# Order of the convolution units and of ScalarE's waits in a convolution-attention-Mamba kernel

## Chip, cores, metric

The kernel runs on one core of a Trainium2 chip. The metric is the device time of one execution in microseconds (us). Engines are named as in the profile: PE (TensorE), DVE (VectorE), ACT (ScalarE), POOL (GpSimd) and SP (SyncE, which here only issues DMAs).

## What is computed

The input is one image of 64 x 64 points with 256 channels. Layer 0 normalises it by groups and computes three convolutions, q, k and v, each followed by a depthwise 3 x 3 convolution; attention over the 4096 points in 8 heads follows. Layer 1 treats the points as tokens: a Mamba block in both directions with a small two-layer network behind it, and then two of eight experts, chosen from the mean of all tokens.

```python
qkv = concat([conv(xc, W1, 0), conv(xc, W3, 1), conv(xc, W5, 2)], axis=1)   # 1x1, 3x3, 5x5
qkv = conv(qkv, Wdw, 1, groups=3 * c)                                       # depthwise 3x3
q, k, v = split(qkv, 3)
q, k = l2n(q), l2n(k)                     # each row of 4096 points is divided by its norm
attn = softmax(q @ k.T * temperature)
...
h = dA_t * h + dBx_t                      # Mamba: for each token, 512 x 16 states, both directions
y = sum_s(h * C_t)
y = (y + xc * Dp) * silu(z)
```

The norm `l2n` runs over the 32 channels of a head at each point. In Mamba dA = exp(dt * A), dBx = dt * B * xc, and z is the second half of the input projection.

## The kernel before

**Three stages matter here**: `conv_phase` (0 to about 682 us), `attention_phase` (to about 1990) and `mamba_phase` (to about 3890); the experts come last. In the first and the third the order of the instructions on each engine is the order in which the program text issues them: nothing reorders them later, and each engine takes its own in order. What runs beside what is therefore decided by where generators are stepped.

**Convolutions.** k and v are Winograd-like convolutions along x: `inputs` (DVE) combines shifted columns of the padded input into transformed planes v0 to v8 ("places", nine of them, taken and freed), `weights` (DVE) combines the raw weights of one row dy into transformed weights in three pieces (two for k), stores them by DMA from POOL into `uv` or `uk`, and PE multiplies. q is 1 x 1 and needs no transform. The work goes by units (kind, half of the image, tile of 128 channels), in the order of the list `units`. Four PSUM buffers (`cv`) hold products; `feed` issues products on PE, up to three ahead of `product`, which hands them out.

For a k or v unit `transform_out` takes the products in pairs: ACT copies the second to `c`, DVE adds and subtracts into `out_t` and combines the rest into `pad`, one of two padded images (a unit uses `pads[n % 2]`). For q `evacuate` copies four products into `pad` on ACT. `sides` then copies the outer columns. `depthwise` of a unit runs while the next unit is made: ACT does tap 0 (L541), DVE the other eight taps of two pieces (L548, 16 instructions). v's result is transposed by PE (`turn`, L612) and copied out by ACT (L614). q's and k's go in sets of three chunks through `norm_sums` (ACT squares, PE sums), `norm_inverse` (DVE reciprocal, 3.35 us, and PE spreading it) and `norm_apply` (DVE), one step for each `tick`. The first half of the image leaves nine rows for the second in `edges`.

In the unit loop each group does, in this order: a step of the unit's own work, `feed`, `tick`, some steps of the depthwise before it, and `share[kind]` steps of `step_fill`, which advances the list `fills`: inputs and weights of k and v that are still to be made. `fills[5]` is `all_weights("v", 1)`: five rows dy in three pieces, 15 pieces.

**Mamba.** There are 16 steps (8 chunks of 512 tokens, two directions), each with 32 slots. A slot n handles two groups of 32 channels times 4 states: POOL makes `dbx` (`inflow`, L1713), ACT makes `da` (`decay`, L1703), DVE scans (`recur`, L1724) and multiplies by C (L1729; in five of 32 slots POOL does it, L1734), PE sums (`sum_states`, L1761), and ACT keeps the last column (`keep`, L1752). In each slot the loop issues `inflow(n + 2)`, `keep(n - 1)`, `decay(n + 1)`, `bring(n + 1)`, `recur(n)`.

A scan covers two channel groups in one instruction, so the state that enters the second is added by `bring` (L1744), a one-column ACT instruction on `dbx`, from `brought`. `carry` makes `brought` in three parts: POOL (L1437), ACT's exp (L1439), POOL (L1442); for the first half of a step in slots 30 and 31 of the step before, for the second in slots 9 to 11. L1437 reads `first_r`, which `load_first` (L1427) loads by DMA through SP from a row (`first_row`, L1414) that `dt_piece` stored. In slot 8 there is one `bring` more, for slot 10:

```python
bring(n + 1)
if at == 8:
    bring(n + 2)
```

`prepare(q)` makes all inputs of step q while step q - 1 runs, one generator step a slot; its last six steps fall into slots 24 to 29. There `zs` (two PSUM tiles of the input projection) is copied to `z` on ACT (L1398), both tiles in slot 24 and both in slot 26, and `load_first(q, 0)` is issued in slot 28, after the second `first_row` store.

Of the kernel before, what the change touches and what calls it, by code (L numbers as in the profile page):

```python
# [14 lines left out]
FP = mybir.dt.float32  # L15
# [9 lines left out]
P = 128  # L25
# [4 lines left out]
N = 512  # L30
# [143 lines left out]
def conv_phase(cx, xT, w1, w3, w5, temp, qd, kd, vd, uk, uv):  # L174
# [13 lines left out]
    nc, tc = cx.nc, cx.tc  # L188
    HR = 32
    LAG = 24  # L190
    TX = W // 4
    with ExitStack() as ctx:
        one = ctx.enter_context(tc.tile_pool(name="a_one", bufs=1))
# [24 lines left out]
        for pad in pads:  # L218
            nc.gpsimd.memset(pad[:, :, 0, 0], 0.0)
            nc.gpsimd.memset(pad[:, :, 5, TX - 1], 0.0)  # L220
        edges = {k: one.tile([P, 9, 6, TX], FP, name=f"edge{i}") for i, k in enumerate((0, 1, "q"))}
        out_t = one.tile([P, 4 * N], FP, name="out_t")
        wq = one.tile([P, CT, C], FP, name="wq")
        for t in range(CT):
# [185 lines left out]


        units = [("k", h, t) for h in range(2) for t in range(CT)]
        units += [("q", 0, 0), ("v", 0, 0), ("v", 0, 1), ("q", 1, 0), ("q", 0, 1), ("q", 1, 1), ("v", 1, 0), ("v", 1, 1)]
        jobs = [
            (u, i) for u in units for i in (range(4) if u[0] == "q" else PTS[u[0]])
        ]
# [1 line left out]
        at = {"load": 0, "job": 0, "used": 0}  # L418
# [81 lines left out]
            yield  # L500

        def sides(pad, r0):
            nc.scalar.copy(pad[:, r0 : r0 + HR, 0, 1:TX], pad[:, r0 : r0 + HR, 4, 0 : TX - 1])
            nc.scalar.copy(pad[:, r0 : r0 + HR, 5, 0 : TX - 1], pad[:, r0 : r0 + HR, 1, 1:TX])

        diag = one.tile([P, 9, P], FP, name="diag")

# [14 lines left out]
        def depthwise(kind, half, t, pad):  # L522

            row0, n = (LAG, H - LAG) if half else (0, LAG)
            ch = {"q": 0, "k": CT, "v": 2 * CT}[kind] + t
            dst = accp.tile([P, (H - LAG) * W], FP, name="acc", tag="acc")
            shared = 16 if (kind, half, t) == units[-1] else 0
            mine = n - shared

            def piece(b, tap):  # L530
                dy, dx = divmod(tap, 3)
                m = mine // 2
                return (
                    dst[:, m * W * b : m * W * (b + 1)].rearrange("p (h w) -> p h w", w=W),
                    pad[:, m * b + dy : m * b + dy + m, dx : dx + 4, :].rearrange("p h s j -> p h (s j)"),
                    wdw[:, 9 * ch + tap : 9 * ch + tap + 1],
                )

            for b in range(2):
                o, src, w_ap = piece(b, 0)  # L540
                nc.scalar.activation(o, src, AF.Copy, scale=w_ap)  # L541
            parts = [pcv.tile([P, N], FP, name="cv", tag="cv") for _ in range(shared // 8)]
            for i, ps in enumerate(parts):
                products(pad, mine + 8 * i, ps)
            for b in range(2):
                for tap in range(1, 9):
                    o, src, w_ap = piece(b, tap)
                    nc.vector.scalar_tensor_tensor(o, src, w_ap, o, ALU.mult, ALU.add)  # L548
                    yield
                if kind == "v":  # L550
                    m = mine * W // P // 2
                    turn(dst, t, row0 * W // P, m * b, m)
                if b == 0 and shared:
                    for i, ps in enumerate(parts):
                        nc.scalar.copy(dst[:, W * (mine + 8 * i) : W * (mine + 8 * i + 8)], ps)
                    turn(dst, t, row0 * W // P, 2 * m, shared * W // P)
            if kind != "v":
                c0 = row0 // ROWS
                rows_left.extend((dst[:, N * j : N * j + N], kind, t, c0 + j) for j in range(n // ROWS))
                if not busy:  # L560
                    norm_sums()

        def norm_sums():

            chunks = rows_left[:3]
            del rows_left[:3]
            busy[:] = chunks
            if not chunks:  # L570
                return
            ps = pms.tile([P, N], FP, name="ps", tag="ps0")
            for j, (a, _, _, _) in enumerate(chunks):
                sq = tp.tile([P, N], FP, name="sq", tag="t")
                nc.scalar.activation(sq, a, AF.Square)
                nc.tensor.matmul(ps[32 * j : 32 * j + 32, :], heads, sq, start=True, stop=True)
            later(lambda: norm_inverse(chunks, ps))
# [44 lines left out]
        def tick():  # L622

            clock[0] += 1
            due = [f for n, f in events if n <= clock[0]]
            events[:] = [(n, f) for n, f in events if n > clock[0]]
            for f in due:
                f()

        with tc.manual_schedule(engines=ORDERED):  # L630
# [68 lines left out]

            pure = fills[1::2]  # L700

            def step_fill():


                held = False
                for f in list(fills):
                    if held and f not in pure:
                        continue
                    r = next(f, None)
                    if r:  # L710
                        return True
                    if r is None:
                        fills.remove(f)
                    else:
                        held = True
                return False


            share = {"k": 5, "q": 4, "v": 3}
            before = None  # L720
            for n, (kind, half, t) in enumerate(units):
                pad, r0 = pads[n % 2], 9 if half else 1
                edge = edges["q" if kind == "q" else t]
                if half:
                    nc.scalar.copy(pad[:, 0:9], edge)
                    nc.gpsimd.memset(pad[:, HR + 9, :, :], 0.0)
                else:
                    nc.gpsimd.memset(pad[:, 0, :, :], 0.0)
                if kind == "q":
                    def evacuate():  # L730
                        for i in range(4):
                            r = r0 + 16 * (i // 2)
                            nc.scalar.copy(
                                pad[:, r : r + 16, 1 + 2 * (i % 2) : 3 + 2 * (i % 2), :],
                                product().rearrange("p (h s j) -> p h s j", s=2, j=TX),
                            )
                        sides(pad, r0)
                        yield

                    main, groups = evacuate(), 1  # L740
                else:
                    main, groups = transform_out(kind, pad, r0), len(PTS[kind]) // 2
                if n == 0:
                    feed()
                    for _ in range(6):
                        step_fill()
                for g in range(groups):
                    step(main)
                    feed()
                    tick()  # L750
                    for _ in range(-(-18 // groups)):
                        step(before)
                    for _ in range(share[kind]):
                        step_fill()
                    feed()
                drain(main)
                drain(before)
                if not half:
                    nc.scalar.copy(edge, pad[:, LAG : LAG + 9])
                before = depthwise(kind, half, t, pad)  # L760
                if n == len(units) - 2:
                    diagonal(2 * CT + units[-1][2])
# [441 lines left out]
def mamba_phase(cx, early, w_in, w_x, w_out, w1, w2, x1d, ud, bcd, dtd, x2d, u2d, usum):  # L1204
# [11 lines left out]
    nc, tc = cx.nc, cx.tc  # L1216
    with ExitStack() as ctx:
# [87 lines left out]
        def prepare(q):  # L1305
# [78 lines left out]
            yield  # L1384
            got["dt"] = dt
            for at, (v, e) in enumerate(((0, 0), (1, 0), (0, 1), (0, 2), (0, 3), (1, 1))):
                dt_piece(q, v, e, ex)
                if at == 4 and q > 1:
                    load_first(q, 0)
                if at == 1:  # L1390
                    zs = in_pair(q, ET + 2)
                    if q + 1 < 2 * NCH:
                        load_u(q + 1)
                if at in (0, 2):
                    z = sp.tile([P, 2, N], FP, name="z", tag="z", bufs=3)
                    got.setdefault("z", []).append(z)
                    for f in range(2):
                        nc.scalar.copy(z[:, f, :], zs[f])  # L1398
                yield

        def dt_piece(q, v, e, ex=None, eng=nc.gpsimd):
# [21 lines left out]
        def load_first(q, h):  # L1423

            t_ = got_first[q, h] = ip.tile([P, 4, 2], FP, name="first_r", tag="first_r", bufs=1)
            rows = first_rows.pop((q, h)).rearrange("(c j) e -> c (j e)", j=4)
            nc.sync.dma_start(out=t_.rearrange("p j e -> p (j e)"), in_=rows[:, None].to_broadcast([32, 4, 8]))  # L1427
# [361 lines left out]
        with tc.manual_schedule(engines=ORDERED):  # L1789
# [5 lines left out]
            for n, (i, e, k, j) in enumerate(slots):  # L1795
# [8 lines left out]
                if n > 0:  # L1804
                    decay(n + 1)
                bring(n + 1)
                if at == 8:
                    bring(n + 2)
                recur(n)
                nxt = (i, e + 1) if e < ET - 1 else (i + 1, 0)  # L1810
                if nxt[0] < 2 * NCH:
# [377 lines left out]
```

## Time and profile before

| | |
|---|---|
| median of 3 runs (lowest, highest) | 4211.03 us (4209.73, 4214.56) |
| profiled execution | 4214.29 us, span 4212.5 us |
| mean granted PE clock | 0.925 |
| PE busy | 3616.6 us (86%) |
| DVE busy | 3493.8 us (83%) |
| ACT busy | 2678.3 us (64%) |
| POOL busy | 1739.0 us (41%) |

The span is from the first to the last instruction of the profiled execution; its own time is 1.8 us longer. Busy shares are means over stages with different limits, so they say little alone: a wait counts only where the waiting engine is the one that sets the pace of its stage. In the profile a group is named by its line and by the tiles written and read ("acc<-pad"); idle time is put down to the instruction that ended it ("<-PE ps L576").

### The profile page before, as it was taken

How to read it: one execution, taken by the hardware profiler on the slowest of the kernel's cores; microseconds unless marked ns; L12 is line 12 of the kernel's file. 1: busy time of each engine (PE TensorE's matmuls, PEld its weight loads, DVE VectorE, ACT ScalarE, POOL GpSimd, SP SyncE). 2: the span in 40 equal slices, each digit the busy share in tenths (PEclk: the TensorE clock that was granted, in tenths of full speed). 3: DMA queues.
4: the chain of work that ended last, by engine and by line, in shares of the span. 5: the costliest groups of instructions: out<-in, count | busy, mean ns of one | idle time of the engine just before them, and what ended most of it. 6: DMA issues, size and time to landing. Idle time of an engine off the chain costs nothing. (4 is left out here: it accounts for less than half of the span.)

```text
span 4212.5 us, 43554 instructions
## 1 busy us (share of the span) xinstructions
PE 3616.6 (86%) x15116; PEld 1182.8 (28%) x15116; DVE 3493.8 (83%) x2898; ACT 2678.3 (64%) x4187; POOL 1739.0 (41%) x1132
## 2 busy tenths in 40 slices
PE   6679698999999999998788788878888888875798
PEld 2223242222222222222222222322222222221343
DVE  8996767879879878778899999999999999999211
ACT  1111315878878878776777777777777777774122
POOL 3200000000000000001888888888888888886000
PEclk9889798999999999999888899989899999977899
DMA  6412124000000000002334343443334443442121
GB/s 208 133 62 89 42 80 140 9 29 19 16 24 19 17 24 19 11 21 85 111 117 122 117 128 114 132 121 117 118 106 128 121 128 117 134 114 72 65 65 39
DMA packets 150532, 351.19 MB, mean 83 GB/s; under 512 B 35493, under 2 KB 44453, under 8 KB 150046
## 3 DMA queue, kind: packets, MB, share of 16 engines
q1 hardware_dynamic: 139214, 313.17, 24.2%
q0 software_dynamic: 11088, 35.14, 2.4%
q8 instruction: 121, 1.98, 0.2%
q14 instruction: 109, 0.89, 0.1%
HBM read 268.69 MB, written 79.56 MB: 83 GB/s over the span
## 5 line engine op out<-in xcount | busy, mean ns | idle before, releaser
L1713 POOL TENSOR_TENSOR dbx<-dtxr,b 128x1024 f32<-128x1024 f32 x512 | 1201.6, 2359 | 202.2 <-DVE da L1724 105.7
L997 ACT ACTIVATE e<-sc 128x1024 f32<-128x1024 f32 x1024 | 992.5, 1023 | 201.7 <-PE sc L990 158.9
L1724 DVE TENSOR_TENSOR_SCAN da<-da,state,dbx 128x1024 f32<-128x1024 f32 x432 | 1014.3, 2348 | 42.9 <-ACT state L1752 21.9
L916 DVE TENSOR_TENSOR s<-s,e 128x1024 f32<-128x1024 f32 x768 | 880.6, 1218 | 44.8 <-ACT e L997 44.3
L1703 ACT ACTIVATE da<-dtr,aneg 128x512 f32<-128x512 f32 x1024 | 708.1, 691 | 31.9 <-DMA dtr<-dtd 2.1
L990 PE MATMUL sc<-q,kS 32*128 32x512 f32 x4096 | 653.4, 643 | 9.9 <-ACT e L997 7.0
L132 POOL TENSOR_TENSOR ln_few<-ln_few,minus_half 128x4 f32<-128x4 f32 x29 | 29.4, 1012 | 1403.3 <-DMA ln_few<-ln_row 1403.3
L1729 DVE TENSOR_TENSOR h<-da,c 128x1024 f32<-128x1024 f32 x432 | 529.2, 1225 | 33.7 <-DVE da L1724 1.4
L923 PE MATMUL av<-e,vT 128*32 128x512 f32 x4096 | 548.4, 606 | 3.7 <-ACT o L929 3.7
L1761 PE MATMUL y<-h,sel 128*32 128x512 f32 x2048 | 380.7, 650 | 99.1 <-DVE h L1729 82.1
L451 PE MATMUL cv<-v,u 128*128 128x512 f32 x928 | 416.5, 609 | 45.4 <-DVE pad L272 26.1
L990 PEld LDWEIGHTS sc<-q,kS 32*128 32x128 f32 x4096 | 211.8, 183 | 454.1 <-issue 226.0
L1287 PE MATMUL mm<-u,win 128*128 128x512 f32 x496 | 254.5, 661 | 79.4 <-ACT z L1398 34.3
L548 DVE SCALAR_TENSOR_TENSOR acc<-pad,wdw_s,acc 128x768 f32<-128x768 f32 (+1 forms) x192 | 235.8, 1234 | 31.8 <-ACT acc L541 26.2
L451 PEld LDWEIGHTS cv<-v,u 128*128 128x128 f32 x928 | 179.1, 195 | 279.9 <-issue 228.9
L1752 ACT COPY state<-da 128x2 f32<-128x2 f32 x431 | 68.1, 158 | 260.7 <-DVE h L1729 260.0
L1333 PE MATMUL mm<-xp,taps 128*128 128x512 f32 x480 | 213.7, 597 | 3.8 <-DVE m L1482 3.7
L916 DVE TENSOR_TENSOR s<-e 128x1024 f32<-128x1024 f32 x128 | 150.9, 1220 | 63.6 <-ACT e L997 63.4
L1724 DVE TENSOR_TENSOR_SCAN h<-da,state,dbx 128x1024 f32<-128x1024 f32 x80 | 187.4, 2343 | 15.7 <-ACT da L1703 9.1
L923 PEld LDWEIGHTS av<-e,vT 128*32 128x32 f32 x4096 | 81.2, 108 | 395.6 <-issue 378.0
L1734 POOL TENSOR_TENSOR h<-h,c 128x1024 f32<-128x1024 f32 x80 | 188.5, 2356 | 2.1 <-ACT state L1752 2.1
L1761 PEld LDWEIGHTS y<-h,sel 128*32 128x32 f32 x2048 | 56.9, 112 | 392.5 <-DVE h L1729 188.1
(351 smaller groups left out, 3892.6 us busy)
## 6 DMA issues: line engine op xcount, KB each, us to landing
dtr<-dtd SPq DMA_DIRECT2D x128, 512.0 KB
dtxr<-dtd SPq DMA_DIRECT2D x128, 512.0 KB
b<-bcd SPq DMA_DIRECT2D x64, 256.0 KB
c<-bcd SPq DMA_DIRECT2D x64, 256.0 KB
dtd<-dt SPq DMA_DIRECT2D x64, 256.0 KB
dtd<-few SPq DMA_DIRECT2D x64, 256.0 KB
u<-uv SPq DMA_DIRECT2D x24, 640.0 KB
u<-ud SPq DMA_DIRECT2D x16, 512.0 KB
```

The costliest lines, as they stand in the source:

```text
L451: nc.tensor.matmul(rows4(ps), u[:, dy, P * ci : P * ci + P], v[:, dy : dy + HR, ci, :], start=dy + ci == 0, stop=dy == k - 1 and ci == CT - 1,
L548: nc.vector.scalar_tensor_tensor(o, src, w_ap, o, ALU.mult, ALU.add)
L916: nc.vector.tensor_tensor(z, x, y, ALU.add)
L923: nc.tensor.matmul(g.av[32 * h : 32 * h + 32, :], vT[:, kb, P * t + 32 * h : P * t + 32 * h + 32], es[h // 2][:, h % 2, :], start=kb == 0, ...
L990: nc.tensor.matmul(ps[h // 2][:, h % 2, :], kS[r, t, P * kb : P * kb + P], q_t[r, t, :], start=True, stop=True,)
L997: nc.scalar.activation(e, ps[i], AF.Exp)
L1287: nc.tensor.matmul(ps, win[d][:, t, P * e : P * e + P], u[:, t, ::-1] if d else u[:, t, :], start=t == 0, stop=t == CT - 1,)
L1703: nc.scalar.activation(da[:, v, :], dts[i, e, j][0][:, v, :], AF.Exp, scale=aneg[i % 2][:, a : a + 1])
L1713: nc.gpsimd.tensor_tensor(u, dts[i, e, j][1], bcs[i, k][0][:, None, :].to_broadcast([P, 2, N]), ALU.mult)
L1724: nc.vector.tensor_tensor_scan(das[n].rearrange("p v n -> p (v n)"), da.rearrange("p v n -> p (v n)"), u.rearrange("p v n -> p (v n)"), st ...
L1729: nc.vector.tensor_tensor(h, da, bcs[i, k][1][:, None, :].to_broadcast([P, 2, N]), ALU.mult)
L1761: nc.tensor.matmul(ys[i, e][32 * j : 32 * j + 32, :], cx.sel, hs[n + j // 2][:, j % 2, :], start=False, stop=k == SQ - 1,)
```

## The change

**Convolutions.** The eight units behind k go in the order q v q v q q v v, where they went q v v q q q v v: q(0,1) comes between v(0,0) and v(0,1), and q(1,0) after v(0,1). As q's two tiles then both wait for their second halves, there are two `edges` tiles for q. `step_fill` holds back `second`, the weights of v's second tile, until the first v product is issued. q units take twelve steps of `step_fill` ahead of the depthwise in place of four behind it. `norm_sums` is begun one tick later. The edges hold only four of six column groups, and `sides` covers the nine rows of the first half as well.

**Mamba.** The extra `bring` of slot 8 goes, so that slot 9 does it as its ordinary one. `load_first(q, 0)` moves from slot 28 to slot 27 and stands before that slot's `dt_piece`. The four copies of `zs` are spread over slots 24 to 27, one in each.

```diff
-        units += [("q", 0, 0), ("v", 0, 0), ("v", 0, 1), ("q", 1, 0), ("q", 0, 1), ("q", 1, 1), ("v", 1, 0), ("v", 1, 1)]
+        units += [("q", 0, 0), ("v", 0, 0), ("q", 0, 1), ("v", 0, 1), ("q", 1, 0), ("q", 1, 1), ("v", 1, 0), ("v", 1, 1)]
...
-        edges = {k: one.tile([P, 9, 6, TX], FP, name=f"edge{i}") for i, k in enumerate((0, 1, "q"))}
+        edges = {
+            k: one.tile([P, 9, 4, TX], FP, name=f"edge{i}") for i, k in enumerate((0, 1, ("q", 0), ("q", 1)))
+        }
...
+            rows = slice(0 if r0 > 1 else r0, r0 + HR)
+            nc.scalar.copy(pad[:, rows, 0, 1:TX], pad[:, rows, 4, 0 : TX - 1])
+            nc.scalar.copy(pad[:, rows, 5, 0 : TX - 1], pad[:, rows, 1, 1:TX])
...
                 if not busy:
-                    norm_sums()
+                    busy.append(None)
+                    later(norm_sums)
...
+            second = fills[5]
...
                 for f in list(fills):
+                    if f is second and at["job"] < first_v:
+                        held = True
+                        continue
...
-            share = {"k": 5, "q": 4, "v": 3}
+            first_v = next(n for n, (u, _) in enumerate(jobs) if u[0] == "v")
+
+            share = {"k": 5, "q": 0, "v": 3}
...
                     step(main)
                     feed()
                     tick()
+
+                    for _ in range(12 if kind == "q" else 0):
+                        step_fill()
                     for _ in range(-(-18 // groups)):
                         step(before)
...
             for at, (v, e) in enumerate(((0, 0), (1, 0), (0, 1), (0, 2), (0, 3), (1, 1))):
+                if at == 3 and q > 1:
+                    load_first(q, 0)
                 dt_piece(q, v, e, ex)
-                if at == 4 and q > 1:
-                    load_first(q, 0)
+                if at in (0, 2):
+                    z = sp.tile([P, 2, N], FP, name="z", tag="z", bufs=3)
+                    got.setdefault("z", []).append(z)
+                if at < 4:
+                    nc.scalar.copy(z[:, at % 2, :], zs[at % 2])
                 if at == 1:
                     zs = in_pair(q, ET + 2)
...
-                if at in (0, 2):
-                    z = sp.tile([P, 2, N], FP, name="z", tag="z", bufs=3)
-                    got.setdefault("z", []).append(z)
-                    for f in range(2):
-                        nc.scalar.copy(z[:, f, :], zs[f])
...
                 bring(n + 1)
-                if at == 8:
-                    bring(n + 2)
                 recur(n)
```

More of the change, by code (lines that the diff above doesn't have):

```diff
@@ L502, in sides @@
         def sides(pad, r0):
-            nc.scalar.copy(pad[:, r0 : r0 + HR, 0, 1:TX], pad[:, r0 : r0 + HR, 4, 0 : TX - 1])
-            nc.scalar.copy(pad[:, r0 : r0 + HR, 5, 0 : TX - 1], pad[:, r0 : r0 + HR, 1, 1:TX])
+            rows = slice(0 if r0 > 1 else r0, r0 + HR)
+            nc.scalar.copy(pad[:, rows, 0, 1:TX], pad[:, rows, 4, 0 : TX - 1])
+            nc.scalar.copy(pad[:, rows, 5, 0 : TX - 1], pad[:, rows, 1, 1:TX])
         diag = one.tile([P, 9, P], FP, name="diag")
@@ L722, in conv_phase @@
                 pad, r0 = pads[n % 2], 9 if half else 1
-                edge = edges["q" if kind == "q" else t]
+                edge = edges[(kind, t) if kind == "q" else t]
                 if half:
-                    nc.scalar.copy(pad[:, 0:9], edge)
+                    nc.scalar.copy(pad[:, 0:9, 1:5, :], edge)
                     nc.gpsimd.memset(pad[:, HR + 9, :, :], 0.0)
@@ L758, in conv_phase @@
                 if not half:
-                    nc.scalar.copy(edge, pad[:, LAG : LAG + 9])
+                    nc.scalar.copy(edge, pad[:, LAG : LAG + 9, 1:5, :])
                 before = depthwise(kind, half, t, pad)
```

## Prediction

> **What bounds the kernel now.** I read the stage windows first, with edges at the places where PE and DVE change roles. Columns: stretch, length, then busy us (count) of PE, PEld, DVE, ACT, POOL, then granted clock, DMA share, GB/s.
>
> ```profile
> 139.20:259.30 120.10, 71.47 (x148) 27.69 (x147) 114.40 (x156) 16.52 (x26) 22.52 (x42) 0.77 0.30 99
> 289.00:404.00 115.00, 114.32 (x291) 48.54 (x290) 80.80 (x89) 14.47 (x24) 7.21 (x14) 1.00 0.28 95
> 404.00:483.70 79.70, 36.12 (x71) 14.01 (x70) 66.39 (x54) 19.04 (x31) 4.70 (x10) 0.66 0.10 33
> 488.80:638.20 149.40, 147.62 (x370) 62.73 (x369) 98.73 (x92) 36.53 (x56) 7.42 (x15) 1.00 0.23 78
> 1995.30:3890.00 1894.70, 1531.33 (x4328) 493.82 (x4328) 1789.93 (x1086) 1435.54 (x2793) 1620.42 (x929) 0.89 0.39 118
> ```
>
> The convolutions (0 to 682 us) have no single bound. DVE sets the k stage; PE sets v(0,0) and v(0,1), with DVE idle for 34 us of 115; DVE sets the three q units after them, with PE idle for 44 us of 80; PE sets the last two v units. Mamba (1995 to 3890) is DVE: 1790 of 1895 us. The timelines of PE and DVE show the places.
>
> ```profile
> 244.93 3.78 PE L443 MATMUL cv<-xpad,wq 128*128 128x512 f32 x4 [18.28 <-DVE pad L272]
> 339.03 0.69 DVE L583 TENSOR_SCALAR rn<-ps 96x512 f32<-96x512 f32 x1 [8.95 <-PE ps L576]
> 458.37 25.31 DVE L548 SCALAR_TENSOR_TENSOR acc<-pad,wdw_s,acc 128x1280 f32<-128x1280 f32 x16 [9.05 <-ACT acc L541]
> 488.81 25.91 PE L451 MATMUL cv<-v,u 128*128 128x512 f32 x60
> ```
>
> The first line is PE waiting 18 us for DVE at the end of the k stage; the second is DVE waiting for PE inside v; the third is the 16 taps of q(1,0), which PE waits for before the first product of v(1,0) (fourth line). So the convolutions end earlier if that 488.8 moves: from there to the end the order of work stays, PE-bound.
>
> For Mamba I took the waits of DVE and ACT from 1800 on (waiter, releaser: total, times, longest).
>
> ```profile
> DVE da L1724 <- ACT state L1752: 21.9, 22, 2.0
> DVE da L1724 <- ACT dbx L1744: 14.0, 14, 4.2
> ...
> ACT brought L1439 <- POOL brought L1437: 40.4, 14, 6.9
> ACT dbx L1744 <- POOL dbx L1713: 20.7, 21, 2.0
> ```
>
> DVE's idle time, sorted by the scan (L1724) that it precedes and summed over the steps: 10.9 us before slot 0, 16.5 before slot 2, 14.5 before slot 10, 3.3 before slot 26. The timelines tell why (POOL, ACT, DVE at a step's end; then ACT and DVE at slots 8 to 10 of step 8).
>
> ```profile
> 3533.07 0.22 POOL L1437 TENSOR_TENSOR brought<-aneg,first_r 128x16 f32<-128x16 f32 x1 [3.37 <-DMA first_r<-first_row]
> 3533.32 0.22 ACT L1439 ACTIVATE brought<-brought 128x16 f32<-128x16 f32 x1 [5.12 <-POOL brought L1437]
> 3536.15 2.36 DVE L1724 TENSOR_TENSOR_SCAN da<-da,state,dbx 128x1024 f32<-128x1024 f32 x1 [2.62 <-ACT dbx L1744]
> ...
> 2978.47 0.29 ACT L1744 ACTIVATE dbx<-dbx,brought 128x1 f32<-128x1 f32 x1 [1.50 <-POOL dbx L1713]
> 2984.85 2.35 DVE L1724 TENSOR_TENSOR_SCAN h<-da,state,dbx 128x1024 f32<-128x1024 f32 x1 [0.90 <-ACT state L1752]
> ```
>
> **What the Trainium skill says.** "PSUM — Partial Sum Buffer", section "Engine vs sequencer instructions": ScalarE's, VectorE's and GpSimd's queues are strict FIFO. The trace agrees: while ACT waits 1.50 us at 2978.47 for the dbx of slot 10, Silu and the decay of slot 10 behind it stand still, and DVE's scan at 2984.85 is late. "TensorE: Matmul & The Clock Gate", Part 1: after some us of idling PE runs at half rate; here four q matmuls take 3.78 us at 244.93 after the idle, 1.88 at 404.25. "DMA: Bandwidth & Descriptors", "Anatomy of one DMA": about 2 us fixed for each transfer; first_r (4 KB), issued at 3526.03, releases POOL at 3533.07, 7.0 us later, so its place among other transfers matters more.
>
> **Convolutions, step by step** (us of the old span; the order of the instructions of both kernels gives what stands where). Durations from the DVE and PE timelines, start to start: a piece of weights 1.93 (six or so operations of 0.42), a tap 1.03 on 768 columns and 1.57 on 1280, a norm 4.7 (0.68, ACT's root 0.70, reciprocal 3.35), a step of v's inputs 2.6, a v product 8.7 on PE (20 records), a k product 5.3.
> (a) K stage. The 15 pieces of v's second weights leave it: 15 x 1.93 (start to start of a piece) = 29, and a 2.3 us wait for their raw load. Its end moves from 259.3 to 228; ACT's squares and first taps, till now beside those pieces, get exposed: +3, so 231. Norms begun a group later cost nothing here: squares and sums are the same in number, the scaled rows leave by DMA and are wanted only by the attention, some 400 us on; without that cover a norm's 4.7 would count.
> (b) Q(0,0). 12 of the pieces come back (23.2) and run dry once on their raw loads (POOL issues each only after the stores of the piece set before: +2.3), then k(1,1)'s 16 taps (25.2): 282. PE starts v(0,0) at 226, when the taps have freed q's pad (before: 256.8), makes 5 products and then idles until the next norm; nothing wanted is late by that, since DVE has a backlog. On POOL the moved weights bring 30 stores (0.54 each) and their raw loads (0.85 each), 20 us in all beside DVE's 29, on a queue that is under 20% busy in these stretches. A memset of k's pad, which waits for those 16 taps, stands ahead of the last 6 stores; these run near 297, and v(0,1)'s first product wants the weights at 331: 34 of cover.
> (c) V(0,0). The DVE rows that stand between (transforms, three norms at 4.7, q(0,0)'s 16 taps, the last 3 pieces) sum to 45.7: 327.5. PE's remaining products end by 315, ahead.
> (d) Q(0,1). Here is a new stall, which the old order couldn't have, as v(0,1) followed v(0,0) at once. Q(0,1)'s evacuation on ACT waits until q(0,0)'s taps have left the same pad, at 327; v(0,1)'s products need the PSUM that it frees. PE: start 331.5, three products 26.2, 2 for the cold clock, norm 1.1, then v(0,0)'s transposes 3.6. Behind these on ACT stand the copy of `edge` and the copy c for v(0,1)'s first pair: 365. DVE has had a norm (6) and 16 taps (16.6), is done at 350 and waits 15.
> (e) V(0,1) with q(0,1)'s taps and the half-1 inputs: DVE rows 71.7: 437.
> (f) Q(1,0). ACT does qo, three squares and only then the tap-0 of v(0,1): +4; 16 taps 16.6: 457.5. Transposes, q(1,1)'s evacuation and its last product: v(1,0) starts 6 later, 463.5.
> Against 488.8: **25 us less**. Q(1,0)'s taps (25.2) now lie beside v(1,0)'s first three products, as q(0,1)'s did. Smaller `edge` copies (0.90 to about 0.6) and longer side copies (0.59 to 0.7) lie on idle ACT. Bounds: without any starving DVE needs 196 us of work after 228, which ends some 50 us earlier than before; with (d) and the ring of small tiles (stores of a set before its buffers return) worse by 15, 10 remain.
>
> **Mamba.** PE, DVE and POOL keep their order; ACT and SP change.
> First load in slot 27: on SP it passes two b/c loads and the second first_row store, about 6 us earlier (3526.0 to 3520); it then lands at 3527 or so, and POOL asks at 3529.7. POOL's own DMA waits at L1437 are 21.3 (19.0 of them on first_r), so ACT's 40.4 falls to about 19, 1.4 a step. Step by step the idle time of DVE in slots 0 and 2 is ACT's wait less 0.9 (5.12: 4.1; 2.65: 1.4; 1.20: 0.5). So 27 falls to 7: **-20**. If the load still came late: 0.
> Slot 8: the early bring waits 1.50 in even steps, 0.54 in odd, ahead of a table load, Silu and decay(10). It goes behind decay(10), where dbx is ready; its 0.28 stays. Even steps lose all of 0.9 (x6), odd ones about 0.6 (x6): **-9** of 14.5.
> Z copies: one of 0.53 goes from slot 24 to 25, from 26 to 27. Slot 26's 0.5 in even steps goes: **-3**. PE's input products wait for the second copy; behind them stand `sum_states`, with four h buffers of slack: 0, at most +5.
> Together -32; a faster DVE meets the waits that stay (xc on PE's y, 13.2 in all), so I take **-28**.
>
> **Sum.** The profiled execution took 4214.3 (span 4212.5 and 1.8 around it), 3.3 above the median 4211.0 of the runs. 4214.3 - 25 - 28 = 4161, or **4158** against that median. A measurement of this kernel can tell about 0.2% (8.4 us) from no change.
>
> **Rivals.**
> 1. Convolutions gain, Mamba doesn't: ACT's lateness has another cause (both table loads, 1.28 each, around Silu in slot 0), and the waits only change names: 4186. Against it: the wait-less-0.9 relation.
> 2. Mamba gains, convolutions don't: (d) and the t buffers eat the 25: 4183. For it: DVE already waits for c copies 20 us.
> 3. Convolutions without the stall in (d), Mamba full: -45 and -32: 4134.
> 4. **Slower**: SP is in order too. In slot 27 the first load waits for its row's store; behind it stand b/c loads and dtr/dtxr of slot 29, wanted some 4 slots later (14.7, less 8 for landing: 6 of slack). Held by w, each of 14 steps loses w - 6; with 53 gained it decides from w = 10 on; at 12 it gives 4158 + 84 = 4242. Against it: the store's issue and the load lie a slot apart, and SP's waits for first_row were 3.5 in all.
> 5. Gains and new stalls cancel: 4211.
>
> **How the numbers follow.** Main 0.59 (own range 4140 to 4176), rival 1 0.12, 2 0.10, 3 0.12, 4 0.04, 5 0.03. Faster: 0.93; same 0.03; slower 0.04. The range 4130 to 4190 takes in the main case with its bounds and most of rivals 1 to 3.
>
> **What would show it.** V(1,0)'s first product near 464 and attention's start near 657; DVE idle before out_t at about 350 to 365 with ACT's c named; the k stage's end near 230; L1437 without DMA waits, L1439's total near 19; DVE idle before slots 0, 2 and 10 below 15 together. It is wrong if v(1,0) starts after 480, if L1437 still waits for first_r, or if POOL or PE take over DVE's waits in Mamba.

## The result, and the profile after

The median went from 4212.8 us (4 runs, one more than in the table above) to 4174.1 us (4 runs, 4172.48 to 4177.76): 38.7 us less, ratio 0.9912 (95% interval 0.9897 to 0.9928). The forecast was 53 us less, 14 more than came. The profiled execution took 4177.76 us (span 4175.9), 36.5 less than the one before. The changed kernel has 13 more lines ahead of Mamba: L1437 is L1450 now, L1439 L1452, L1713 L1726, L1724 L1737, L1744 L1757.

First the stage windows, with edges where PE and DVE change roles now (k stage, q(0,1), v(0,1), last two v units, Mamba; columns as before):

```profile
139.20:230.50 91.30, 68.97 (x165) 28.41 (x164) 87.43 (x81) 18.07 (x27) 3.63 (x8) 0.87 0.21 68
...
322.00:364.80 42.80, 40.86 (x111) 17.05 (x110) 27.55 (x28) 11.51 (x22) 4.16 (x9) 1.00 0.27 95
364.80:408.50 43.70, 43.70 (x109) 18.56 (x108) 42.53 (x45) 6.48 (x10) 2.21 (x5) 1.00 0.25 88
...
461.90:611.30 149.40, 147.96 (x369) 63.20 (x367) 106.10 (x91) 36.20 (x54) 7.05 (x15) 0.99 0.22 76
1968.30:3850.00 1881.70, 1533.84 (x4326) 492.69 (x4328) 1787.31 (x1086) 1435.50 (x2793) 1620.74 (x929) 0.89 0.38 119
```

The k stage is 29 us shorter. In q(0,1) DVE works only 27.55 us of 42.80 while PE is busy; in v(0,1) both are busy nearly all the time, where DVE was busy for only 80.80 of the 115 us of v(0,0) and v(0,1) in the old order. The last stretch is as long as before, 149.4 us. Mamba's DVE idles 94 us, where it idled 105.

The timelines of DVE and PE in the convolutions:

```profile
285.09 1.28 DVE L277 TENSOR_TENSOR out_t<-cv,c 128x512 f32<-128x512 f32 x2
...
334.88 3.35 DVE L589 RECIPROCAL rn<-rn 96x512 f32<-96x512 f32 x1 [3.49 <-ACT rn L588]
...
364.82 1.29 DVE L277 TENSOR_TENSOR out_t<-cv,c 128x512 f32<-128x512 f32 x2 [10.07 <-ACT c L482]
...
439.33 16.70 DVE L551 SCALAR_TENSOR_TENSOR acc<-pad,wdw_s,acc 128x768 f32<-128x768 f32 x16 [3.47 <-ACT acc L544]
...
461.89 18.29 PE L453 MATMUL cv<-v,u 128*128 128x512 f32 x40
```

The third line is the forecast's new stall, at its place and with ACT's `c` named; the last is v(1,0)'s first product, 26.9 us earlier than before. Attention starts at 656.8 (before: 682.6).

In Mamba the waits of POOL, ACT, DVE and SP (total, times, longest):

```profile
POOL dbx L1726 <- DMA dtxr<-dtd: 100.4, 39, 16.5
...
DVE da L1737 <- ACT state L1765: 25.6, 16, 2.7
...
ACT dbx L1757 <- POOL dbx L1726: 21.1, 14, 3.5
ACT brought L1452 <- POOL brought L1450: 20.9, 14, 2.2
...
SPq L1440 <- DMA first_row<-first: 59.7, 17, 5.2
```

The 40.4 us that ACT waited for `brought` have become 20.9, and POOL waits for `first_r` no more (19.0 before). But POOL's wait for `dtxr` is 100.4 where it was 73.2, and SP now waits 59.7 us for the `first_row` store, where it waited 3.5. POOL's waits for `dtxr` in slot 0 alone (between the scans of slots 0 and 1) rose from 4.1 to 23.9 us, and DVE's idle time in slots 0 to 2 did not fall: 27.4 before, 28.8 after. The same step as before (a step's end, then the new step's slots 0 to 2; SP, POOL, ACT and DVE) shows the chain:

```profile
3487.67 0.59 SPq L1473 DMA_DIRECT2D dtxr<-dtd  x1
...
3489.75 0.22 POOL L1450 TENSOR_TENSOR brought<-aneg,first_r 128x16 f32<-128x16 f32 x1
...
3495.03 9.29 POOL L1726 TENSOR_TENSOR dbx<-dtxr,b 128x1024 f32<-128x1024 f32 x4 [2.56 <-DMA dtxr<-dtd]
...
3497.41 0.29 ACT L1757 ACTIVATE dbx<-dbx,brought 128x1 f32<-128x1 f32 x1 [1.92 <-POOL dbx L1726]
3497.73 1.28 ACT L1848 ACT_TABLE_LOAD   x1
...
3504.05 2.36 DVE L1737 TENSOR_TENSOR_SCAN da<-da,state,dbx 128x1024 f32<-128x1024 f32 x1 [2.69 <-ACT state L1765]
```

`first_r` is there in time, so POOL goes on at once, and then stands 2.56 us for the `dtxr` of slot 1, which SP issued in slot 29 (first line). ACT's `bring` of slot 1 waits 1.92 behind it, and all that ACT has to do next, both table loads, Silu and the decay of slot 2, moves back by as much; DVE pays 2.69 us ahead of slot 2 in place of 2.62 ahead of slot 0.

### The profile page after: what moved, and what is told of

Its sections match the earlier page's. It is cut to its first block, busy times and chain, and to the rows that moved or that the text cites. A ratio compares the mean times of both kernels' runs of the same rounds, so it can differ in the third digit from the quotient of the medians.

```text
span 4175.9 us, 43561 instructions
## 1 busy us (share of the span) xinstructions
PE 3613.0 (87%) x15116; PEld 1180.8 (28%) x15116; DVE 3491.8 (84%) x2898; ACT 2676.0 (64%) x4187; POOL 1738.8 (42%) x1132
## 3 DMA queue, kind: packets, MB, share of 16 engines
q1 hardware_dynamic: 139214, 313.17, 23.9%
## 5 line engine op out<-in xcount | busy, mean ns | idle before, releaser
L1726 POOL TENSOR_TENSOR dbx<-dtxr,b 128x1024 f32<-128x1024 f32 x512 | 1201.6, 2358 | 231.2 <-DVE da L1737 109.0
L1737 DVE TENSOR_TENSOR_SCAN da<-da,state,dbx 128x1024 f32<-128x1024 f32 x432 | 1014.1, 2347 | 40.3 <-ACT state L1765 25.6
L1737 DVE TENSOR_TENSOR_SCAN h<-da,state,dbx 128x1024 f32<-128x1024 f32 x80 | 187.4, 2342 | 3.6 <-ACT dbx L1757 2.4
```

The lines of the kernel that those rows point to most:

```text
L1726: nc.gpsimd.tensor_tensor(u, dts[i, e, j][1], bcs[i, k][0][:, None, :].to_broadcast([P, 2, N]), ALU.mult)
L1737: nc.vector.tensor_tensor_scan(das[n].rearrange("p v n -> p (v n)"), da.rearrange("p v n -> p (v n)"), u.rearrange("p v n -> p (v n)"), st ...
```

## The experiments

Times are compared with the kernel before on the same chip (medians of 4215 to 4223 us there), as a ratio with its 95% interval, but for experiments 9 and 10, which have one execution each. DVE's idle time by slot comes from the DVE timeline of one profiled execution of each kernel, summed over all steps but the first; POOL's and ACT's likewise.

**1. Convolutions alone.** Everything from `mamba_phase` on as before.

> Convolution part of the change alone; Mamba as before. Theory (the two parts add up, and the convolutions carry two thirds of the gain): 26 us below the kernel before, v(1,0)'s first product at 462, the first attention scores at 657, Mamba's 16 steps as long as before. Rival (the parts are not independent: the conv part also shifts Mamba's transfers): the difference is under 20 or over 32 us although attention starts at 657.

Measured: 4205.3 against 4223.4, ratio 0.9958 (0.9944 to 0.9972), so 18 us (12 to 24). In its profile v(1,0) starts at 464.0 and attention at 659.0, 23.6 us earlier than before; but from its first scores to Mamba's first scan 1321 us passed, where the three other kernels of this chip had 1316. The conv part moves the start of attention by 24 to 26 us; the whole runs show less, with an interval whose upper end just reaches that. The rival's "under 20" was met by the time, and it is not ruled out as a cause: DVE's idle time in slots 0, 2 and 10 of Mamba is 15.5, 17.6 and 14.1 us, where the kernel before had 10.9, 16.5 and 14.5, and the 14 steps took 1658 us in place of 1654. But that profile of the kernel before is from another chip, and experiment 2 shows longer steps on this one without the conv part, so what ate the rest is left open.

**2. Mamba alone.** Everything up to `mamba_phase` as before.

> Mamba part of the change alone; convolutions as before. Theory: 13 us below the kernel before, all of it from slots 8 to 10 and 26 (DVE's idle time ahead of slot 10 falls from 14.5 to about 2.4 us, ahead of slot 26 from 3.3 to 0), while the idle time of DVE in slots 0 to 2 stays near 28 us. Rival (the forecast's sum was right and the changed kernel's profile shows a poor draw): 28 us below.

Measured: ratio 0.9976 (0.9966 to 0.9985), so 10 us (6 to 14). The forecast's 28 is outside. DVE's idle time ahead of slot 10 is 2.6 us and ahead of slot 26 none; in slots 0 to 2 it is 34.9. So the profile of the changed kernel was no poor draw.

**3. Load_first back in slot 28**, all else as changed:

```diff
-                if at == 3 and q > 1:
-                    load_first(q, 0)
                 dt_piece(q, v, e, ex)
+                if at == 4 and q > 1:
+                    load_first(q, 0)
```

> The changed kernel with load_first(q, 0) back in slot 28, behind its dt_piece; all else as changed. Theory (the earlier load brought nothing net, because the dbx of slot 1 then waits for its dtxr): within 4 us of the changed kernel, POOL's wait for first_r back at about 19 us and its wait for dtxr in slot 0 down from 24 to about 4. Rival 1 (the earlier load brought the forecast's 20 us and something else ate it): 10 to 20 us slower than the changed kernel. Rival 2 (the earlier load costs, since SP waits 60 us for the first_row store and b, c, dtr and dtxr leave later): 5 to 10 us faster than the changed kernel.

Measured: 4190.4, ratio 0.9927 (0.9914 to 0.9941). The changed kernel's ratio was 0.9912, and 0.9909 (0.9896 to 0.9922) on a third chip (experiment 5): 6 to 8 us apart, with intervals that overlap. POOL waits 18.7 us for `first_r` again, and its wait for `dtxr` in slot 0 is 3.5. On this chip DVE idles 36.7 us in slots 0 to 2 here and 34.9 in experiment 2, which has the early load. The time lies between the theory and rival 1 and speaks against the 20; experiment 11 tests the load by itself. Against experiment 1, on the same chip and with the same convolutions, it is 15 us faster: slot 8's `bring` and the spread copies, forecast at 9 + 3.

**4. Dtxr ahead of dtr**, the rest as changed:

```diff
-            for v, nm in enumerate(("dtr", "dtxr")):
+            for v, nm in ((1, "dtxr"), (0, "dtr")):
...
-                tiles.append(t_)
+                tiles.insert(0, t_)
```

> The changed kernel with the two loads of load_dt exchanged: dtxr is issued ahead of dtr. Theory (after the change DVE's idle time in slots 0 to 2 hangs on dtxr, which is queued behind dtr's 512 KB): dtxr is issued 0.6 us earlier and lands 2 to 3 us earlier, POOL's wait for dtxr in slot 0 falls from 24 to under 5 us, DVE's idle time in slots 0 to 2 from 29 to about 12, the kernel is 15 us faster than the changed one (4159). Rival 1 (SP stands still for the first_row store, that sets the landing): dtxr gains 0.6 us and the time stays within 5 us. Rival 2 (dtr is now late for decay): ACT waits for dtr, DVE for da, slower by 5 us or more.

Measured: 4170.2 against 4223.4, ratio 0.9873 (0.9858 to 0.9888): 53 us below the kernel before, 16 more than the changed kernel's ratio gives. Against experiment 3, which lacks both this edit and the early load, it is 20 us faster on the same chip. POOL's waits on `dbx`, by what ended them:

```profile
  DVE da L1737: 157.2, 124
  DVE h L1737: 17.7, 28
  DMA dtxr<-dtd: 12.5, 10
```

For `dtxr` 12.5 us are left of 83.1 (the changed kernel's 100.4 without the two waits ahead of Mamba's first scan, which lie outside this answer); POOL now waits for DVE, which is the bound. In slot 0 they are 5.3 of 23.9, and DVE's idle time in slots 0 to 2 is 14.0 of 28.8. Where POOL waited for the `dtxr` of slot 1, its `dbx` began 7.8 us after the issue in the changed kernel (median of 11 steps) and 6.9 here (8 steps), beside the 0.6 us of earlier issue: 1.5 together. Part of rival 2 is there too: ACT now waits 7.1 us for `dtr` in slot 0, half as much as DVE's idle time that is left.

**5. The changed kernel again**, beside the next three.

> The changed kernel itself, beside the next three on one chip. Both theories: about 37 us below the kernel before, DVE's idle time in slots 0 to 2 near 29 us.

Measured: 4179.6 against 4218.7, ratio 0.9909 (0.9896 to 0.9922), 39 us less. DVE idles 27.2 us in slots 0 to 2.

**6. Dtxr first, and load_first in slot 28** (the edits of 3 and 4 together).

> The changed kernel with dtxr loaded ahead of dtr and load_first(q, 0) back in slot 28. Theory (two late arrivals stand behind each other at POOL, first_r and dtxr; each taken away alone gives little, both together give what the forecast had for one): POOL waits for first_r again, about 19 us, ACT's L1452 about 40, DVE's idle time in slots 0 to 2 about 30, and the kernel is 12 us slower than with dtxr first and load_first early. Rival (dtxr alone was the late one): within 4 us of that kernel.

Measured: 4178.0, ratio 0.9901 (0.9889 to 0.9914), 12 us worse than experiment 4 by the ratios, as the theory had it. POOL at `first_r`'s instruction (L1450):

```profile
  DMA dtr<-dtd: 9.2, 3
  DMA first_r<-first_row: 8.0, 6
```

17 us of waiting are back there, ACT's wait for `brought` is 35.4, and DVE idles 23.2 us in slots 0 to 2, a little under the 30 expected. So the earlier load is worth some 12 us once `dtxr` comes first, and the two late transfers stood one behind the other. The other half of the theory, that each edit alone gives little, does not hold for `dtxr`: this kernel and that of experiment 3 differ in `dtxr`'s place alone, and their ratios lie 11 us apart (0.9901 and 0.9927, on two chips, the intervals just touching), with DVE's idle time in slots 0 to 2 at 23.2 and 36.7 us.

**7. Transposes a tick later** (on top of 4):

```diff
-                    turn(dst, t, row0 * W // P, m * b, m)
+                    if shared:
+                        turn(dst, t, row0 * W // P, m * b, m)
+                    else:
+                        later(lambda b=b, m=m: turn(dst, t, row0 * W // P, m * b, m))
```

> The changed kernel with dtxr ahead of dtr, and in the convolutions v's transposes put off by one tick (except in the last unit), so that the copy c for the next v unit's first pair stands ahead of the copies vs on ACT. Theory (DVE's 10 us of waiting at 354.8 is ACT's c, which stands behind vs copies and so behind PE's transposes and products): out_t starts at 355 in place of 364.8, v(1,0) at 454 in place of 462, attention 8 us earlier, kernel 8 us faster than with dtxr first alone. Rival (another wait takes its place: DVE then waits for PE's products or the ring of small tiles): v(1,0) at 460 or later, time within 3 us.

Measured: ratio 0.9945 (0.9933 to 0.9956), 30 us slower than 4. The theory's first half holds: `out_t` starts at 358.5 with no wait, right behind the taps. But the transposes then stand on PE behind two more products and a norm, the copies `vs` on ACT behind the transposes, and q(0,1)'s tap 0 on ACT behind the copies. ScalarE's queue is strict FIFO, as the Trainium skill has it ("PSUM — Partial Sum Buffer", "Engine vs sequencer instructions"), and here are 26 us of that (DVE, ACT and PE timelines):

```profile
386.88 5.24 DVE L551 SCALAR_TENSOR_TENSOR acc<-pad,wdw_s,acc 128x768 f32<-128x768 f32 x5 [21.76 <-ACT acc L544]
...
382.19 0.58 ACT L621 COPY vs<-tr 128x512 f32<-128x512 f32 x1 [26.44 <-PE tr L619]
...
385.90 1.76 ACT L544 ACTIVATE acc<-pad,wdw_s 128x768 f32<-128x768 f32 x2
...
381.50 0.66 PE L619 MATMUL tr<-ident,acc 128*128 128x128 f32 x4
```

10 us of waiting turned into 22, and v(1,0) starts at 475.8, 14 us later than in experiment 4. The last two v units then take 169 us in place of 149. A worse wait than the rival's took its place.

**8. Norms begun at once**, as before:

```diff
-                    busy.append(None)
-                    later(norm_sums)
+                    norm_sums()
```

> The changed kernel with norms begun at once, as before. Theory (forecast: the delay by a group costs nothing by itself, and gains nothing): v(1,0) starts within 3 us of 462, time within 4 us of the changed kernel. Rival (the delay is what takes the norm's waits for PE and ACT off DVE's path): v(1,0) starts 5 us later or more.

Measured: v(1,0) starts at 467.9, 6 us later than beside it in experiment 5, attention at 667.9, 13 later; ratio 0.9925 (0.9912 to 0.9938) against 0.9909. The rival holds on v(1,0), so the delay is no neutral edit there in the new order; of the time 7 us show, but the two intervals overlap.

**9 and 10. Old order with the rest of the change; new order with weights and shares of fills as before.** One run each, for the places in the convolutions.

```diff
# 9
-        units += [("q", 0, 0), ("v", 0, 0), ("q", 0, 1), ("v", 0, 1), ("q", 1, 0), ...]
+        units += [("q", 0, 0), ("v", 0, 0), ("v", 0, 1), ("q", 1, 0), ("q", 0, 1), ...]
# 10
-                    if f is second and at["job"] < first_v:
+                    if False:
...
-            share = {"k": 5, "q": 0, "v": 3}
+            share = {"k": 5, "q": 4, "v": 3}
...
-                    for _ in range(12 if kind == "q" else 0):
+                    for _ in range(0):
```

> The changed kernel with the old order of units (q v v q q q v v); weights still held back, norms later. Theory (the two edits need each other: the held-back weights start v early, and only the new order keeps DVE busy beside v): v(0,0) starts near 220, v(1,0) at 475 to 485. Rival (holding back the weights is the whole gain): v(1,0) at 466 or earlier.

> The changed kernel with the new order of units, but v's second weights not held back and q's share of fills as before (four behind the depthwise). Theory (as for the old order): v(0,0) starts near 257, as before, and v(1,0) at 470 to 480. Rival (the order is the whole gain): v(1,0) at 466 or earlier.

V(1,0)'s first product, in PE's timeline of 9 and of 10:

```profile
481.96 18.32 PE L453 MATMUL cv<-v,u 128*128 128x512 f32 x37 [22.91 <-ACT pad L743]
```

```profile
463.77 25.91 PE L453 MATMUL cv<-v,u 128*128 128x512 f32 x60
```

The old order keeps PE waiting 22.9 us ahead of v(1,0), as the theory had it. But the order, with the later norms (and the smaller edges, which no run takes back), gives 25.0 of the 26.9 us, although v(0,0) starts only at 253: my expectation of 470 to 480 was wrong and the rival right. Holding back the weights is worth 2 us at v(1,0), and none at the start of attention, 656.6 in 10 and 656.8 in the changed kernel. In 9 attention starts at 694.3, later than before the change, and PE waits there for the load of k's scaled rows:

```profile
694.26 3.78 PE L1003 MATMUL sc<-q,kS 32*128 32x512 f32 x12 [8.03 <-DMA kS<-kd]
```

K's own stores were issued by 414.8. SP's timeline has this load at 687.2, behind a wait for PE's last product of q's last norm (L594, 684.2 to 686.2): in this order the last norm has no cover left (4231.2 us in its one run, beside 4221.1 for the kernel before).

**11. Load_first in slot 27 alone**, on the kernel before (the reverse of 3's edit).

> The kernel before with one edit: load_first(q, 0) in slot 27, ahead of its dt_piece. Theory (the dbx of slot 1 then waits for dtxr, so the wait only changes its name): within 6 us of the kernel before; POOL's waits for first_r fall from about 19 to 0, its waits for dtxr in slot 0 rise from 4 to 20 to 30, DVE's idle time in slots 0 to 2 stays within 5 us of its 27, and SP waits about 60 us for the first_row store. Forecast's step: 20 us faster, DVE's idle time in slots 0 and 2 down to 7.

Measured: 4214.8 against 4215.0, ratio 0.9998 (0.9990 to 1.0006). POOL's `dbx`, and SP's wait at the load:

```profile
  DMA dtxr<-dtd: 92.3, 36
```

```profile
SPq L1427 <- DMA first_row<-first: 61.6, 18, 5.2
```

Of the 92.3 us one wait of 17.6 lies at Mamba's start. POOL never waits for `first_r`, ACT's L1439 waits 19.4 us in place of 40.4, and POOL's wait for `dtxr` in slot 0 is 19.3 in place of 4.1. DVE idles 23.3 us in slots 0 to 2, and 8.1 in place of 6.4 ahead of slot 24. The step forecast at 20 us is worth 0, within 4 us either way.

**12. Third product behind the transposes** (on top of 4):

```diff
                     step(main)
-                    feed()
+                    if kind != "q":
+                        feed()
                     tick()
```

> The changed kernel with dtxr loaded ahead of dtr, and in q units without the feed ahead of tick, so that the third product of the next unit stands behind the transposes on PE. Theory (DVE's 10 us of waiting at 354.8 is the third product, 8.7 us, that PE makes ahead of the transposes): out_t starts at 359 in place of 364.8, v(1,0) at 457 in place of 462, 5 us faster than with dtxr first alone, so about 58 below the kernel before. Rival (PE has no slack in v(0,1) and gives the 5 us back by the last product): v(1,0) at 461 or later, time within 3 us of dtxr first alone.

Measured: 4158.5 against 4215.0, ratio 0.9866 (0.9851 to 0.9881), 57 us below the kernel before. It is the lowest of all ratios and stands clear of the changed kernel's, but not of experiment 4's. The 58 expected were met in time without their reason (DVE's timeline, then PE's):

```profile
354.69 1.29 DVE L277 TENSOR_TENSOR out_t<-cv,c 128x512 f32<-128x512 f32 x2 [4.08 <-ACT c L482]
373.31 1.29 DVE L277 TENSOR_TENSOR out_t<-cv,c 128x512 f32<-128x512 f32 x2 [2.54 <-ACT c L482]
382.30 0.69 DVE L587 TENSOR_SCALAR rn<-ps 96x512 f32<-96x512 f32 x1 [5.16 <-PE ps L580]
...
461.53 17.33 PE L453 MATMUL cv<-v,u 128*128 128x512 f32 x40
```

The stall fell from 10.1 to 4.1 us, so the third product was indeed in front of the transposes. Then DVE waits twice more, 2.54 us for ACT's copy `c` and 5.16 for PE, which works without a gap from 353.0 to 392, and v(1,0) starts where it did: the rival is right. In the changed kernel's v(0,1) PE was busy 43.70 and DVE 42.53 of 43.70 us, so neither had slack to give.

## Why the prediction was right, and where it failed

**Convolutions, 25 forecast, 26 measured** at the start of attention (18, 12 to 24, of the whole time in experiment 1). Step by step, forecast and measured: (a) end of the k stage 231, 230.5. (b) Q(0,0) done at 282, 285.1; DVE ran dry 5.7 us on the stores of weights and 0.65 on a raw load, where 2.3 was put. (c) 327.5, 329.6. (d) 365, 364.8; the wait for `c` was 10.1, not 15, because DVE was done at 354.8, not 350: 2.1 us came from (c), the rest from a norm that waited 4.6 us for PE and ACT, so that the 15 us of the stall were 5 too many and its end right. (e) 437, 435.9. (f) The exposed tap 0 cost 3.5, not 4, and v(1,0) started at 461.9, not 463.5. The order of instructions together with durations start to start was enough for these places. What the chain of places could not tell is which edit brings it: the order with the later norms 25.0, the held-back weights 2 on top. And "norms begun a group later cost nothing" was half the answer: without the delay v(1,0) starts 6 us later (experiment 8), and in the old order, with the delay, the last norm ended so late that attention started 11.7 us later than in the kernel before (experiment 9); the old order with the rest of the change but without the delay was not tried.

**Mamba, 28 forecast; 13.3 measured over the 14 whole steps** (1653.8 to 1640.5 us in the profiles). Slot 8's `bring`: forecast 9, DVE's idle time ahead of slot 10 fell by 12.1 (14.5 to 2.4). Z copies: forecast 3, slot 26 fell by 3.3; slot 24 rose by 3.4 (6.4 to 9.8). Slot 24's figure was 7.0 to 13.6 with the early load (experiments 2, 5 and 8 to 11), 6.9 and 7.0 with the late one (3 and 1), and 9.8 or 6.4 with `dtxr` first (4, 6, 12 and 7); what makes it was not tried.

The step that failed is "**so 27 falls to 7: -20**". All that it says up to POOL came true: no wait for `first_r`, L1439 at 20.9 (19 forecast). The error is the rule drawn from the trace of before, that DVE's idle time in slots 0 and 2 is ACT's wait less 0.9. It held while `first_r` came last. The second `dbx` behind L1437 on POOL needs a `dtxr` that SP issues after the load. In the step that the forecast shows of the kernel before, it was there only 9.1 us after its issue (SP's timeline, then POOL's):

```profile
3527.33 0.59 SPq L1460 DMA_DIRECT2D dtxr<-dtd  x1
...
3536.41 9.29 POOL L1713 TENSOR_TENSOR dbx<-dtxr,b 128x1024 f32<-128x1024 f32 x4 [0.62 <-DMA dtxr<-dtd]
```

POOL waited 0.62 us for it, and would have waited more, had `first_r` not held it for 3.37 first. Asked what is late next, the forecast named PE's y (13.2 us) and not this transfer, and put the alternative as "if the load still came late: 0". The load came in time and the answer was 0 all the same. The forecast's own sign, DVE's idle time before slots 0, 2 and 10 below 15 together, was missed with 26.1 us, and POOL took over the wait; in these slots rival 1's "the waits only change names" is what happened. With `dtxr` first as well the 20 us are there (experiments 3 and 4).

A second term of that step was off as well: the load was to leave 6 us earlier, and left 1.4 earlier (medians of 14 steps, counted from slot 24's scan), because SP has to wait for the store of its row. This is rival 4's mechanism, at some 4 us a step (56 more over 14 steps). It did not decide, as `dtxr` was issued only 0.4 us later against that scan. But the "6 of slack" of that rival was wrong. It counts 14.7 us to the use of the loads of slot 29; POOL makes `dbx` two slots ahead, and in the changed kernel it was free for this one 5.7 us after the issue (median of 14 steps) and had to wait in 11 of the 14. So this transfer had no slack. That POOL still had `first_r` in time goes with its place ahead of b and c, which no run changed alone.

**The sum.** In the profiles the conv part and attention gave 27.0, Mamba's first step took 0.2 more, the 14 steps gave 13.3, and the rest took 3.5 more: 36.6, the difference of the two spans. What the last 3.5 are was not looked at; the profiled run stands 3.7 above its median. The parts measured alone give less than the whole: experiments 1 and 2 give 18 and 10 us, experiments 3 and 11 give 31 and 0, where the changed kernel has 37 to 38. The intervals allow it, and what the other 6 to 9 us are is left open. The total of 4174 lies 16 us above the forecast's 4158 and 12 below rival 1's 4186, so the time alone does not tell the two apart; the places in the profile do. That it is still inside the main case's own range, which ended at 4176, is in part luck.

## What to carry to other kernels

When a wait is taken away, ask what the same engine needs one and two instructions later and when that arrives: a transfer that came 0.6 us after the end of a 3.4 us wait is the next bound, not a rounding error. Of two transfers that arrive late one behind the other, the first can measure as nothing when it alone is mended (experiment 11) and be worth 12 us once the second is mended too (experiments 4 and 6); test them alone and together. Moving an instruction that another waits for pays only if every in-order queue between them, PE's and ACT's here, has nothing longer to put in front of it.

## What the runs showed of the hardware

In the changed kernel, where POOL waited for the `dtxr` (512 KB) of a step's slot 1, `dbx` began 7.8 us after the issue (median of 11 places), with b and c issued shortly ahead of it; at other waits of Mamba it was 5.8 us (26 places). The small load of `first_r` (4 KB) took 7.1 us in the kernel before, behind b and c (median of the 9 steps where POOL waited for it); ahead of them POOL used it 6.3 us after the issue (median of 14 steps) and never waited. Mamba's 14 steps with the same instructions ran 1638 to 1641 us on two chips (the changed kernel, experiments 5 and 8), 1648 on a third (9 and 10) and 1651 on a fourth (2), in one profiled execution each; on the fourth DVE's idle time in slots 0 to 2 was 6 to 8 us longer than in the changed kernel and in experiment 5. So the chip can count as much as an edit where an arrival decides.
